# Splitting a unit's value products into three runs instead of two

## The chip, the cores and the metric

The kernel runs on one core of one Trainium2 chip. The metric is device time in microseconds: the time of one execution of the whole kernel. Five engines matter here: TensorE (PE in the profile, its weight loads PEld), VectorE (DVE), ScalarE (ACT), GpSimd (POOL) and SyncE (SP), which here issues the transfers.

## The reference

A batch of 4 sequences of 1024 tokens, each with 1024 channels, goes through attention with 16 heads of 64 channels, and then through a causal convolution. All of it is in float32.

```
scale, shift = split(emb @ W_emb + b_emb)
xn     = rms_norm(x, g_norm) * (1 + scale) + shift
q,k,v  = heads(xn @ W_qkv)
q, k   = rms_norm(q, g_q), rms_norm(k, g_k)
attn   = softmax(q @ k.T * d**-0.5)
o      = attn @ v
x      = x + o + o @ W_out          # attention and its residual
out    = x + causal_conv(x, 4 taps from cond) + b
```

What the change touches is the middle: the scores `q @ k.T`, the softmax over the keys, and the product of the weights with `v`, called the value product below.

## The kernel before

**Tiling.** Two heads of 64 channels make a pair and share the 128 partitions. A sequence has 8 pairs. The work on one pair and one half of its queries (512 of 1024) is a *unit*, so there are 4 x 8 x 2 = 64 units, and the main loop at the end of the kernel passes once for each. They are counted from 0 here.

**One unit.** The keys of a sequence are 8 tiles of 128. For each key tile, `Unit.scores` (L629) multiplies keys by queries for both heads, one head in rows 0 to 63 of TensorE and the other in rows 64 to 127, into one PSUM tile `s` of 128 x 1024; the pool of these tiles, `ps_s`, has two buffers. ScalarE copies the tile to SBUF as `sp` (L637), from a pool of nine, and VectorE keeps a running maximum over the tiles, `mx` (L646). When all eight have come, GpSimd takes the maximum over the partitions (L651), ScalarE puts it into PSUM as `mbp` (L660), in a buffer of that same pool of two, VectorE subtracts it from each tile (L665), ScalarE takes the exponential (L669), and GpSimd adds the tiles up as `sum` (L671). `Unit.values` (L692) then multiplies the eight tiles of weights by `v` into one PSUM tile `pav`, both heads side by side in TensorE's columns. `Unit.finish` (L707) multiplies `sum` by ones for the totals `tot`. The totals go through a scratch in DRAM and come back as reciprocals, by which `divide` (L747) scales `pav`.

**Overlap of units.** The softmax of a unit takes long on VectorE, ScalarE and GpSimd. So a unit's value products stand in the next pass of the loop, between the scores of the next unit: `last` is the unit before. In each pass the scores go out in four groups of two key tiles. After each group `fill()` runs a stretch of other work that is due: products of the projections to q, k and v (L589, a scheme with seven products in place of eight), of the output projection (L881, L950), transposes, loads and stores. `split` cuts this work into four stretches. It puts what lies within the last 26 us by its estimate (20 in the first sequence) into the fourth stretch, after the scores, so in most passes the first three stretches hold nothing.

**What sets the order.** The order of TensorE's instructions is that of the calls in the main loop. The other engines' instructions are issued through `defer(delay, key, step)`: a step is put on a list with a due time on the planner's own clock, and `tick(us)` moves that clock and runs what has come due. `scores` and `values` tick by `PAIR`, 0.9, for each key tile. So where calls change places, the clock stands elsewhere between them, and steps that come due there are issued at another place of their engine's queue. Among the deferred steps are those of `Pair`: `squares` (L437, ScalarE), `sums` (L443, VectorE), `root` (L446, a square root on ScalarE, with a load of its table) and `scale` (L451, VectorE), which normalise q and k of a coming pair. [...] Semaphores keep data and buffers safe.

**Buffers around the change.** Score tile `kt` needs the buffer of tile `kt - 2` in `ps_s`, so it waits for ScalarE's copy of that tile. The copy into `sp` number `kt` takes, in the pool of nine, the place of tile `kt - 1` of the unit before, so it needs that unit's value product `kt - 1` to be done.

Of the kernel before, what the change touches and what calls it, by code (L numbers as in the profile page):

```python
# [21 lines left out]
def kernel(  # L22
# [36 lines left out]
    NT = N // P  # L59
    HN = N // 2  # L60
    HT = NT // 2
# [34 lines left out]
    def defer(delay, key, step):  # L96
        pending.append((clock[0] + delay, next(serial), key, step))
# [42 lines left out]
    def need(*key):  # L140
        flush(lambda e: e[2] == key)
# [616 lines left out]
    def gather(b, half):  # L758

        for kh in range(2):  # L760

            n = KH - kh if b == B - 1 else KH
            for k in range(n):
                need("oT", b, kh * KH + k, half)
            if half:
                four = apool.tile([P, 8, QN], F32, tag="r", name=f"ob_{b}_{kh}_{half}", bufs=2)
                four = four.rearrange("p i t -> p (i t)").rearrange("p (k t) -> p k t", t=HN)
            else:
                four = apool.tile([P, KH, HN], F32, tag="ob", name=f"ob_{b}_{kh}_{half}", bufs=2)
            nc.sync.dma_start(four[:, :n, :], scrO[b][half][:, kh * KH : kh * KH + n, :])  # L770
            for k in range(n):
                oTs[b, kh * KH + k, half] = four[:, k, :]
# [403 lines left out]
    def between(p):  # L1176

        b, i = divmod(p, NB)
        slots = [[] for _ in range(7)]
        for j in range(7):  # L1180
            T = 7 * (p + 4) + j
            slots[j] = piece(T) if T < ND * NPR + 16 else []
        slots[0].append((0.0, lambda: store(AGE)))
        d, k = divmod(p - 11, NB)
        if 0 <= d < B - 1 and k % 2 == 0 and k < NJ:
            slots[0].append((0.0, lambda: OutSums(d, k // 2).load()))
        for a, g in enumerate(range(products_until(p), products_until(p + 1))):
            slots[(2, 5)[a]] += out_product(g)
        if p in REST_PLAN:
            at = sum(n for q, n in REST_PLAN.items() if q < p)  # L1190
            for m in REST[at : at + REST_PLAN[p]]:
                slots[6] += [(0.0, lambda: store(AGE_REST))] + out_pieces(m)
                slots[6].append((0.0, lambda m=m: late.append((clock[0], outs[m].store))))
        return [piece for slot in slots for piece in slot]

    def cut(pieces, shares):

        ends = list(accumulate(shares))
        total = sum(t for t, _ in pieces)
        stretches, done = [[] for _ in shares], 0.0  # L1200
        for t, step in pieces:
            at = (done + t / 2) / max(total, 1e-9) * ends[-1]
            stretches[next((i for i, e in enumerate(ends) if at < e), len(ends) - 1)].append((t, step))
            done += t
        return stretches

    def run(pieces):
        for t, step in pieces:
            until = clock[0] + t
            step()  # L1210
            if until > clock[0]:
                tick(until - clock[0])

    def split(pieces, behind):

        left, n = behind, len(pieces)
        while n and left > 0:
            n -= 1
            left -= pieces[n][0]
        return cut(pieces[:n], SHARES) + [pieces[n:]]  # L1220
# [30 lines left out]
    last = None  # L1251
    for p in range(B * NB):
        unit = Unit(doubles[p // 4].pairs[p // 2 % 2], p % 2)
        stretches = split(between(p), BEHIND if p >= NB else BEHIND_FIRST)
        if p == B * NB - 1:


            gather(B - 1, 0)
            gather(B - 1, 1)
            stretches = cut(between(p), SHARES) + [own]  # L1260
        stretches = iter(stretches)

        def fill():
            run(next(stretches))

        unit.scores((0, 1))
        if last is not None:
            need("exp", last.name)
            last.values(range(0, HT))
        fill()  # L1270
        unit.scores((2, 3))
        fill()
        unit.scores((4, 5))
        if last is not None:
            last.values(range(HT, NT))
            last.finish()
        fill()
        unit.scores((6, 7))
        need("mx", unit.name)
        unit.softmax()  # L1280
        if last is not None:
            defer(2.7 if p > B * NB - 2 else DIVIDE, ("oT", last.pr.b, last.pr.c, last.half), last.divide)
        fill()
        last = unit
# [46 lines left out]
```

## Time and profile before

| what | value |
|---|---|
| time, median of 3 runs | 2895.81 us (2890.95 to 2898.24) |
| the profiled execution | 2907.69 us, span of the profile 2905.7 us |
| TensorE clock granted | 0.99 |
| busy: PE, DVE, ACT, POOL | 2793.5, 2182.2, 1695.1, 1345.1 us |
| value products (L692) | 2048 matmuls, 605 ns mean |
| scores (L629) | 2048 matmuls, 623 ns mean |
| score copies (L637) | 512, 1016 ns mean |
| running maxima (L646) | 448, 1328 ns mean for the 384 after the first of each unit |
| subtraction (L665) | 512, 1213 ns mean |
| product for q, k, v (L589) | 3504 matmuls of 128x384, 493 ns mean |

The profile is of one execution on the chip. Times are in microseconds unless marked ns. A float32 matmul shows as two records, so a score tile of two heads is four records. Matmuls are pipelined and their ends are modelled, so lengths of neighbours overlap by up to 0.16 us; the distance from start to start is the better measure. A timeline line gives the start, the length, the engine, the line of the kernel, the operation, output<-inputs, the shape, and how many instructions were merged; brackets hold the engine's idle time before it and what ended that. In a list of waits, a line gives who waited for whom, microseconds in total, times, and the longest.

### The profile page before, as it was taken

How to read it: one execution, taken by the hardware profiler on the slowest of the kernel's cores; microseconds unless marked ns; L12 is line 12 of the kernel's file. 1: busy time of each engine (PE TensorE's matmuls, PEld its weight loads, DVE VectorE, ACT ScalarE, POOL GpSimd, SP SyncE). 2: the span in 40 equal slices, each digit the busy share in tenths (PEclk: the TensorE clock that was granted, in tenths of full speed). 3: DMA queues.
4: the chain of work that ended last, by engine and by line, in shares of the span. 5: the costliest groups of instructions: out<-in, count | busy, mean ns of one | idle time of the engine just before them, and what ended most of it. 6: DMA issues, size and time to landing. Idle time of an engine off the chain costs nothing.

```text
span 2905.7 us, 32179 instructions
## 1 busy us (share of the span) xinstructions
PE 2793.5 (96%) x10529; PEld 1317.5 (45%) x10529; DVE 2182.2 (75%) x2652; ACT 1695.1 (58%) x2269; POOL 1345.1 (46%) x534
## 2 busy tenths in 40 slices
PE   7999999999999999999999999999999999999999
PEld 3544444444444544544444444454444444444344
DVE  3578878888878776787787777787787868788763
ACT  3165657765556666665565666765565656556532
POOL 1045555555455544445544553544553555545520
PEclk9999999999999999999999999999999999999999
DMA  7864455755445656655655564765565445432433
GB/s 278 286 203 135 151 169 177 226 171 163 140 151 189 210 163 199 217 178 186 203 173 166 191 201 141 238 210 179 181 215 172 145 147 178 151 111 87 131 105 116
DMA packets 416255, 510.98 MB, mean 176 GB/s; under 512 B 41889, under 2 KB 327897, under 8 KB 406361
## 3 DMA queue, kind: packets, MB, share of 16 engines
q1 hardware_dynamic: 416088, 508.93, 54.0%
q8 instruction: 84, 1.38, 0.2%
q14 instruction: 83, 0.67, 0.1%
HBM read 413.43 MB, written 95.40 MB: 175 GB/s over the span
## 4 chain that ended last, share of the span: by engine, by line
PE 69%; DVE 14%; ACT 7%; DMA 5%; issue 3%; POOL 1%; SPq 1%; DVEq 0%; ACTq 0%; POOLq 0%
PE pqkv_P L589 27%; PE pav L692 14%; PE s L629 13%; PE po L950 5%; DVE mx L646 5%; PE po_P L881 4%; PE po L881 3%; ACT sp L637 3%; DVE sp L665 3%; ACT sp L669 2%; DMA scrR<-few 1%; DMA rec<-scrR 1%; DVE r L321 1%; PE qkt L459 1%; PE tot L707 1%
## 5 line engine op out<-in xcount | busy, mean ns | idle before, releaser
L589 PE MATMUL pqkv_P<-w_P,a 128*128 128x384 f32 x3504 | 1198.2, 493 | 29.3 <-issue 9.3
L671 POOL TENSOR_TENSOR sum<-sum,sp 128x1024 f32<-128x1024 f32 x384 | 956.1, 2490 | 62.1 <-ACT sp L669 31.6
L589 PEld LDWEIGHTS pqkv_P<-w_P,a 128*128 128x128 f32 x3504 | 652.0, 191 | 505.5 <-issue 91.8
L637 ACT COPY sp<-s 128x1024 f32<-128x1024 f32 x512 | 512.6, 1016 | 489.1 <-PE s L629 385.8
L646 DVE TENSOR_TENSOR mx<-mx,sp 128x1024 f32<-128x1024 f32 x384 | 510.0, 1328 | 174.6 <-ACT sp L637 146.3
L665 DVE TENSOR_TENSOR sp<-sp,mbp 128x1024 f32<-128x1024 f32 x512 | 605.0, 1213 | 18.1 <-ACT mbp L660 18.1
L669 ACT ACTIVATE sp<-sp 128x1024 f32<-128x1024 f32 x512 | 527.6, 1056 | 147.2 <-DVE sp L665 143.1
L651 POOL PARTITION_ALL_REDUCE mb<-mx x64 | 220.5, 3445 | 839.0 <-DVE mx L646 662.6
L629 PE MATMUL s<-qT,kT 64*128 64x512 f32 x2048 | 519.7, 623 | 38.0 <-ACT sp L637 22.8
L692 PE MATMUL pav<-sp,v 128*64 128x512 f32 x2048 | 473.9, 605 | 0.0
L671 POOL TENSOR_TENSOR sum<-sp,sp 128x1024 f32<-128x1024 f32 x64 | 151.3, 2364 | 493.3 <-ACT sp L669 218.9
L629 PEld LDWEIGHTS s<-qT,kT 64*128 64x128 f32 x2048 | 170.0, 186 | 337.9 <-issue 172.6
L692 PEld LDWEIGHTS pav<-sp,v 128*64 128x64 f32 x2048 | 137.2, 138 | 322.0 <-issue 314.3
L986 DVE SCALAR_TENSOR_TENSOR y<-x,cols,y 128x512 f32<-128x512 f32 x192 | 248.0, 1296 | 46.8 <-ACT y L974 42.2
L646 DVE TENSOR_TENSOR mx<-sp,sp 128x1024 f32<-128x1024 f32 x64 | 110.5, 1727 | 104.2 <-ACT sp L637 104.2
L608 DVE TENSOR_TENSOR qk<-u,pqkv_P 128x256 f32<-128x256 f32 x256 | 106.8, 417 | 89.7 <-PE pqkv_P L589 85.3
L950 PE MATMUL po<-ob,wo 128*128 128x512 f32 x352 | 155.3, 593 | 0.0
L881 PE MATMUL po_P<-o_P,wq_P 128*128 128x512 f32 x320 | 143.9, 592 | 0.0
L660 ACT COPY mbp<-mb 128x1024 f32<-128x1024 f32 x64 | 65.2, 1019 | 116.5 <-POOL mb L651 116.4
L451 DVE TENSOR_TENSOR qk<-qk,ms 128x1024 f32<-128x1024 f32 x64 | 125.9, 1968 | 2.2
L881 PE MATMUL po<-o_P,wq_P 128*128 128x512 f32 x240 | 108.0, 592 | 0.0
L437 ACT ACTIVATE sq<-qk 128x512 f32<-128x512 f32 x128 | 76.7, 629 | 52.2 <-DVE qk L608 48.1
(96 smaller groups left out, 1886.2 us busy)
## 6 DMA issues: line engine op xcount, KB each, us to landing
a<-scrA SPq DMA_DIRECT2D x215, 512.0 KB
w_P<-scrB SPq DMA_DIRECT2D x64, 768.0 KB
o_P<-scrS SPq DMA_DIRECT2D x40, 1024.0 KB
w_P<-in_L_cond_W_qkv_dram SPq DMA_DIRECT2D x144, 256.0 KB
o_P<-scrO SPq DMA_DIRECT2D x30, 1024.0 KB
scrA<-r SPq DMA_DIRECT2D x28, 896.0 KB
wq_P<-scrW SPq DMA_DIRECT2D x70, 256.0 KB
xc<-in_x_dram SPq DMA_DIRECT2D x64, 256.0 KB
```

The source lines that it names most:

```text
L589: nc.tensor.matmul(pm, (chunks[0, k].r(place) if a is None else a[:, k, :])[:, t % 2 * P : (t % 2 + 1) * P], w[:, k, :], start=(k == 0), s ...
L629: nc.tensor.matmul(ps[:, h, :], pr.kT[kt // HT][h * D : (h + 1) * D, kt % HT * P : (kt % HT + 1) * P], pr.qT[self.half][h * D : (h + 1) * ...
L637: nc.scalar.copy(sp, ps)
L646: nc.vector.tensor_max(self.mx, self.mx if kt > 1 else self.sp[0], self.sp[kt])
L651: nc.gpsimd.partition_all_reduce(self.mb.rearrange("p h q -> p (h q)"), self.mx.rearrange("p h q -> p (h q)"), P, bass_isa.ReduceOp.max,)
L665: nc.vector.tensor_sub(self.sp[kt], self.sp[kt], self.mb)
L669: nc.scalar.activation(sp, sp, AF.Exp)
L671: nc.gpsimd.tensor_tensor(self.sum, self.sum if kt > 1 else self.sp[0], sp, ALU.add)
L692: nc.tensor.matmul(self.pav[h * D : (h + 1) * D, :], self.pr.v[kt // HT][:, kt % HT, h * D : (h + 1) * D], self.sp[kt][:, h, :], start=(kt ...
L881: nc.tensor.matmul(pm, self.w[name][:, k, :], self.o[name][:, k, :], start=(k == 0 and name not in ("P2", "P3", "P4")), stop=(k == KH - 1),)
L950: nc.tensor.matmul(self.pm, self.w[kh][:, k % KH, :], oTs[b, k, half], start=False, stop=(k == NJ - 1),)
L986: nc.vector.scalar_tensor_tensor(self.y, self.x1[:, k : k + HN], cols[:, r : r + 1], self.y, ALU.mult, ALU.add)
```

## The change

In each pass with a predecessor, the second half of its value products, tiles 4 to 7, stood in one run behind scores 4 and 5. Tiles 4 and 5 now stand ahead of scores 4 and 5, after the second `fill()`; tiles 6 and 7, and the totals, stay where they were. The first half, tiles 0 to 3, stays behind scores 0 and 1. The last unit, whose value products come after the loop in one run, is as before.

```diff
         fill()
         unit.scores((2, 3))
         fill()
+        if last is not None:
+            last.values(range(4, 6))
         unit.scores((4, 5))
         if last is not None:
-            last.values(range(HT, NT))
+            last.values(range(6, NT))
             last.finish()
         fill()
         unit.scores((6, 7))
```

`HT` is 4 and `NT` is 8. `values` opens the PSUM tile `pav` when its first key tile is 0, and closes the accumulation at tile 7, so a run may be cut anywhere between.

## The prediction

> **What bounds the kernel now.** I read the page first (busy shares, the chain that ended last), then the list of waits, then the timeline of single units in each engine. Units are counted from 0, one per pass of the main loop (64 passes).
>
> ```profile
> span 2905.7 us, 32179 instructions
> PE 2793.5 (96%) x10529; PEld 1317.5 (45%) x10529; DVE 2182.2 (75%) x2652; ACT 1695.1 (58%) x2269; POOL 1345.1 (46%) x534
> ...
> PE 69%; DVE 14%; ACT 7%; DMA 5%; issue 3%; POOL 1%; SPq 1%; DVEq 0%; ACTq 0%; POOLq 0%
> ```
>
> TensorE is busy 96% of the span and carries 69% of the chain; the rest of the chain is mostly VectorE. What TensorE waits for, from the list of waits:
>
> ```profile
> PE s L629 <- ACT sp L637: 22.8, 63, 3.1
> PE s L629 <- DVE sp L665: 15.0, 10, 3.4
> ```
>
> 63 waits of the scores for ScalarE's copies, about one a unit. Where they sit shows in the timeline of TensorE in unit 34 (start, length, then the instructions merged):
>
> ```profile
> 1531.68 1.99 PE L629 MATMUL s<-qT,kT 64*128 64x512 f32 x8
> 1533.60 3.65 PE L692 MATMUL pav<-sp,v 128*64 128x512 f32 x16
> 1537.18 1.99 PE L629 MATMUL s<-qT,kT 64*128 64x512 f32 x8
> 1539.48 2.04 PE L629 MATMUL s<-qT,kT 64*128 64x512 f32 x8 [0.31 <-ACT sp L637]
> 1541.46 3.65 PE L692 MATMUL pav<-sp,v 128*64 128x512 f32 x16
> 1545.04 0.64 PE L707 MATMUL tot<-sum,ones 128*32 128x256 f32 x8
> ```
>
> Score tiles 0 and 1, four tiles of the predecessor's values, score tiles 2 to 5 without a break, four tiles of values, the totals. Tile 4 needs the PSUM buffer of tile 2 (the scores have two), and ScalarE copies it out only at
>
> ```profile
> 1538.42 1.93 ACT L637 COPY sp<-s 128x1024 f32<-128x1024 f32 x2 [2.62 <-PE s L629]
> 1540.71 1.01 ACT L637 COPY sp<-s 128x1024 f32<-128x1024 f32 x1 [0.37 <-PE s L629]
> ```
>
> The first of the two copies ends near 1539.43, and tile 4 starts at 1539.48.
>
> **What the Trainium skill says.** "TensorEngine Tiling (Array Packing)", section Key Properties: changing the tiling mode, not only the tile, drains TensorE. The trace agrees: scores (64*128) and values (128*64) are different modes, and a block costs more than its tiles (below). The same page, section PSUM Bottleneck: tiling speeds TensorE but not the evacuation of PSUM; here a score tile's matmuls take 0.86 us and its copy 1.01. "TensorE: Matmul & The Clock Gate", on engine queue depths: ScalarE and VectorE are strict FIFO. I use this for the copies queued behind a waiting square root; the trace shows ScalarE's instructions in program order.
>
> **The change, part by part.** It moves values 4 and 5 of the predecessor ahead of scores 4 and 5. No instruction is added or removed, and values 6, 7 and the totals stay behind scores 5. Single matmuls in the trace start in pairs, a pair every 0.429 us, two pairs a tile: 0.858. A block of two score tiles lasts 1.92 (1531.68 to 1533.60), so entering and leaving it costs 1.92 - 1.72 = 0.20. Four value tiles last 3.58 (1533.60 to 1537.18): 3.43 and 0.15. Two value tiles then last 1.72 + 0.15 = 1.87.
>
> *An ordinary unit.* Before: scores 2 to 5 4.28 (1537.18 to 1541.46) + values 3.58 = 7.86. After: 1.92 + 1.87 + 1.92 + 1.87 = 7.58. So 0.65 of stall goes, 0.35 of two mode changes comes, 0.28 is left. Tile 4 now starts 3.79 after tile 2, and tile 2's buffer is free 2.25 after it, tile 3's 3.2 after it: neither wait is left, with 1.5 us over. Scores 6 start 3.4 after scores 5, their buffer free after 2.3: no new wait there.
>
> *What is queued behind.* Scores 4 and 5 start 1.5 us later, so their copies (ScalarE) and running maxima 4 and 5 (VectorE) do too. This hides in VectorE's idle time before maximum 6 (2.24 us in unit 34), or under its backlog; in every ordinary unit I worked through, maximum 5 still ends before copy 6 arrives. The copy of tile 5 no longer waits for value 4 (0.91 in unit 34); nothing waited for that copy.
>
> *Where the gain passes.* 63 units have a predecessor. In four (24, 25, 40, 41) a product already stands between scores 3 and 4: no stall to remove; a product-to-values change and a values-to-scores change replace a product-to-scores one, about +0.16 each, +0.6 in all. Of the other 59, eight keep nothing. In 2, 6, 14, 16 and 60 maximum 6 starts late behind VectorE's other work, and the next unit's second score tile waits for VectorE's last subtraction: TensorE arrives earlier and waits longer. In 5 and 63 the totals wait for GpSimd's sum (2.57 and 2.54), and after 62 scores wait 3.10 for ScalarE. Elsewhere TensorE sets the pace, or VectorE's chain starts at copy 6 and moves with it.
>
> *The moved square root.* By the order of ScalarE's instructions in the changed kernel, the square root of the norms (L446, with its table load) moves from behind copies 4 and 5 to ahead of them in units 4, 8, ... 60 (24 and 40 had it there). It waits for VectorE's sums (L443). Unit 52, VectorE and then ScalarE before:
>
> ```profile
> 2301.28 6.38 DVE L986 SCALAR_TENSOR_TENSOR y<-x,cols,y 128x512 f32<-128x512 f32 x3
> 2307.58 1.27 DVE L443 TENSOR_REDUCE ms<-sq 128x8 f32<-128x512 f32 x2
> ```
>
> ```profile
> 2304.78 1.01 ACT L637 COPY sp<-s 128x1024 f32<-128x1024 f32 x1 [0.37 <-PE s L629]
> 2306.70 1.01 ACT L637 COPY sp<-s 128x1024 f32<-128x1024 f32 x1 [0.91 <-PE pav L692]
> 2307.74 1.28 ACT L446 ACT_TABLE_LOAD   x1
> 2309.03 0.31 ACT L446 ACTIVATE ms<-ms,eps 128x16 f32<-128x16 f32 x1
> ```
>
> Unit 52 begins at 2295.75. The sums end 13.1 after that; root 0.31 and copy 4 1.01 end at 14.65, so scores 6, due at 13.64 and formerly at 13.92, start near 14.7: +0.8. Unit 8 (sums at 15.9, scores 6 formerly at 16.3): to 17.3, +1.0. Unit 60 (13.4): +0.9, which falls into the 1.17 that the next unit's scores wait for VectorE anyway. In the other ten of these units the sums end 6.6 to 10.4 after the start; copy 4 is due at 10.5 to 10.9 and has 2 us to spare before scores 6: free.
>
> *Sum.* 59 - 8 - 2 = 49 units x 0.28 = 13.7; four of them (21, 22, 37, 38) stall 0.05 less (-0.2), 9 and 33 stall more (+0.44): 14.0. Less 0.6 and 1.8: **11.5 us off**. The profiled execution took 2907.7 us with a span of 2905.7, 0.4% over the median of 2895.8; a saving of a few tenths in each unit is the same in both. 2895.8 - 11.5 = **2884.3**.
>
> The least certain price is the block of two values, which no trace shows alone. Its lower bound is 1.79, half of the block of four, were the extra mode changes free (gain about 0.43 a unit, 21 us over 49 units, 18 net). Its upper bound: I allow both changes to cost half as much again (0.53), leaving 0.10 a unit, 5 us, 2.5 net. I take 1.87, as the same two changes stand around every block of values.
>
> **The rivals.**
> *Absorbed further.* In units 1 to 18 VectorE and TensorE wait for each other often (the second score tile is late by up to 3.6 us), and a copy that comes 1.5 later can delay a maximum there. If these 18 gave nothing, about 13 x 0.28 = 3.6 less and 1 for unit 8: 7 to 8 us off, 2888; with the dearer mode change 2893. For it: VectorE's 14% of the chain. Against: in ten of those units VectorE idles just before maximum 6 (0.9 to 3.0).
> *More than counted.* Mode changes nearly free, or the relief of copy 5 helps ScalarE: 18 us off, 2878. Against: the 0.20 and 0.15 are in every unit.
> *Slower: the square root holds the copies.* Place: the fifteen units named, ahead of copy 4. Price: for each microsecond that the sums end after 12.3 from the unit's start, scores 6 are one later. It decides when the ten harmless units see their sums at about 13.5 (as in unit 52): 10 x (0.28 + 0.8) = 11, all of the gain. At 14.5 each loses 1.8 rather than gaining 0.28, 21 us: 2884 + 21 = 2905. Against: their sums end by 10.4, and VectorE's order hardly changes (two units in which the sums move earlier).
> *Nothing happens.* Excluded as to order: in every unit with a predecessor, two and two value tiles stand around scores 4 and 5. As to time it is the first rival.
>
> **How the numbers follow.** Forecast (9 to 15 us off, 2881 to 2887) 0.58; more than counted 0.10; absorbed 0.26; slower 0.06. About 0.3%, 8.7 us, is what a measurement can tell from no change: faster 0.58 + 0.10 = 0.68, less 0.01 for the edge: 0.67; same 0.27; slower 0.06. The range for 8 in 10 takes in the absorbed case to 2892 and the nearly free mode change to 2878; the forecast's own range is 2881 to 2887.
>
> **What would show it.** From the start of score tile 2 to that of tile 6: 8.42 before, 8.14 after in ordinary units. Score waits for ScalarE's copies: from 22.8 us in 63 to 6 to 9 in about 8 (unit 0, which has no predecessor, keeps three), a new one of 0.6 to 1.2 in units 8, 52 and 60. Waits of scores for VectorE's subtraction up by 1 to 2 us. A two-tile block of values longer than 1.9, or tile-6 waits in the other ten units of the square root, would make it wrong.

## The result, and the profile after

The changed kernel takes 2882.35 us, median of 6 runs (2878.57 to 2884.86), beside 2896.4 us for 6 runs of the kernel before (2890.95 to 2900.51). The ratio is 0.9951, with a 95% interval of 0.9938 to 0.9964: 14 us less, with an interval of 10 to 18. The forecast was 2884.3, 11.5 us less than the median of 2895.81 that was then known.

The page of the changed kernel, its head and the shares of the chain that ended last:

```profile
span 2881.0 us, 32179 instructions
PE 2790.8 (97%) x10529; PEld 1315.6 (46%) x10529; DVE 2184.3 (76%) x2652; ACT 1684.7 (58%) x2269; POOL 1348.2 (47%) x534
...
PE 74%; DVE 12%; ACT 6%; DMA 4%; issue 3%; POOL 2%; SPq 1%; DVEq 0%; ACTq 0%; POOLq 0%
```

TensorE has as much to do as before and waits less, so its share of the chain grows from 69% to 74%. The two spans differ by 24.7 us, more than the medians: the execution of the kernel before that was profiled was 11 us over its median, and this one (2883.05 us) is close to its own. I come back to that below.

The list of waits (who waited for whom, microseconds in total, times, the longest):

```profile
PE s L629 <- DVE sp L665: 12.4, 9, 2.8
...
PE s L629 <- ACT sp L637: 6.9, 7, 3.5
```

The waits of the scores for ScalarE's copies went from 22.8 us in 63 to 6.9 in 7. Unit 34 shows how, in the timeline of TensorE (start, length, then the instructions merged):

```profile
1520.22 1.99 PE L629 MATMUL s<-qT,kT 64*128 64x512 f32 x8
1522.14 1.94 PE L692 MATMUL pav<-sp,v 128*64 128x512 f32 x8
1524.01 1.99 PE L629 MATMUL s<-qT,kT 64*128 64x512 f32 x8
1525.92 1.94 PE L692 MATMUL pav<-sp,v 128*64 128x512 f32 x8
1527.79 0.64 PE L707 MATMUL tot<-sum,ones 128*32 128x256 f32 x8
```

and in that of ScalarE:

```profile
1521.45 1.93 ACT L637 COPY sp<-s 128x1024 f32<-128x1024 f32 x2 [2.62 <-PE s L629]
1525.24 1.93 ACT L637 COPY sp<-s 128x1024 f32<-128x1024 f32 x2 [1.86 <-PE s L629]
```

From start to start, scores 2 and 3 last 1.92, values 4 and 5 1.87, scores 4 and 5 1.91, values 6 and 7 1.87: the four numbers of the prediction's working. The second of the two copies that scores 4 and 5 need ends at 1523.38, and scores 4 start at 1524.01, so no wait is left. From score tile 2 to score tile 6 it is 8.14 (1520.22 to 1528.36), where it was 8.42.

### The profile page after: what moved, and what is told of

It reads as the page before. It is cut to its first block, busy times and chain, and to the rows that moved or that the text cites. A ratio compares the mean times of both kernels' runs of the same rounds, so it can differ in the third digit from the quotient of the medians.

```text
span 2881.0 us, 32179 instructions
## 1 busy us (share of the span) xinstructions
PE 2790.8 (97%) x10529; PEld 1315.6 (46%) x10529; DVE 2184.3 (76%) x2652; ACT 1684.7 (58%) x2269; POOL 1348.2 (47%) x534
## 4 chain that ended last, share of the span: by engine, by line
PE 74%; DVE 12%; ACT 6%; DMA 4%; issue 3%; POOL 2%; SPq 1%; DVEq 0%; ACTq 0%; POOLq 0%
PE pqkv_P L589 28%; PE s L629 14%; PE pav L692 14%; PE po L950 5%; PE po_P L881 4%; DVE mx L646 4%; PE po L881 3%; DVE sp L665 2%; ACT sp L669 2%; ACT sp L637 1%; PE qkt L459 1%; PE tot L707 1%; DMA rec<-scrR 1%; DVE r L321 1%; DMA scrR<-few 1%
## 5 line engine op out<-in xcount | busy, mean ns | idle before, releaser
L589 PE MATMUL pqkv_P<-w_P,a 128*128 128x384 f32 x3504 | 1192.9, 491 | 27.7 <-issue 9.9
L589 PEld LDWEIGHTS pqkv_P<-w_P,a 128*128 128x128 f32 x3504 | 649.8, 191 | 500.3 <-issue 85.8
L637 ACT COPY sp<-s 128x1024 f32<-128x1024 f32 x512 | 505.6, 1016 | 467.9 <-PE s L629 417.2
L629 PE MATMUL s<-qT,kT 64*128 64x512 f32 x2048 | 516.3, 620 | 19.5 <-DVE sp L665 12.4
L692 PE MATMUL pav<-sp,v 128*64 128x512 f32 x2048 | 487.0, 608 | 0.0
L629 PEld LDWEIGHTS s<-qT,kT 64*128 64x128 f32 x2048 | 174.8, 186 | 311.1 <-issue 200.8
L692 PEld LDWEIGHTS pav<-sp,v 128*64 128x64 f32 x2048 | 131.4, 138 | 333.1 <-issue 323.2
L608 DVE TENSOR_TENSOR qk<-u,pqkv_P 128x256 f32<-128x256 f32 x256 | 106.4, 416 | 82.5 <-PE pqkv_P L589 80.7
```

Of the source, the lines that this page charges most:

```text
L589: nc.tensor.matmul(pm, (chunks[0, k].r(place) if a is None else a[:, k, :])[:, t % 2 * P : (t % 2 + 1) * P], w[:, k, :], start=(k == 0), s ...
L629: nc.tensor.matmul(ps[:, h, :], pr.kT[kt // HT][h * D : (h + 1) * D, kt % HT * P : (kt % HT + 1) * P], pr.qT[self.half][h * D : (h + 1) * ...
L637: nc.scalar.copy(sp, ps)
L692: nc.tensor.matmul(self.pav[h * D : (h + 1) * D, :], self.pr.v[kt // HT][:, kt % HT, h * D : (h + 1) * D], self.sp[kt][:, h, :], start=(kt ...
```

## The experiments

Distances between score tiles are from start to start in the trace of TensorE. "The middle" of a unit is from score tile 2 to score tile 6.

**Both kernels once more.** Without an edit, to see which differences belong to one execution.

> The kernel before once more, unchanged, for a second profile. Theory (TensorE's order decides, the rest is run to run): from unit 20 on, start to start of score tiles 2 and 6 is 8.42 us in ordinary units as in the first profile; what differs from the first profile lies in units 0 to 19 and in stretches of 3.4 us at half clock after a long wait. If the extra gains of the changed kernel in units 23, 31, 35 and 39 (0.8 to 1.7 us each) belong to the change, this profile shows the long times of the first one there; if they are run to run, some of them are gone here too.

> The changed kernel again, without an edit. Theory: 2882 again, 14 us below the kernel before; from score tile 2 to tile 6 8.14 in the same units as in its first profile. What belongs to the one execution that was profiled, and not to the change, differs: the stretches at half of TensorE's clock lie elsewhere and in another number (9 to 13 of them in the executions of the two kernels so far), and the differences in units 13 to 19, 31 and 35 between the first two profiles don't return alike. Rival (those differences belong to the change): they return in the same units with the same sizes.

The kernel before took 2896.98 us in its second profiled execution. The changed kernel took 2881.28 us (5 runs, 2879.42 to 2883.78) beside 2897.04 for the kernel before (11 runs), ratio 0.9945 (0.9927 to 0.9962). The middles of the ordinary units are 8.42 and 8.14 again, to 0.01; only unit 2 of the changed kernel was at 8.43 in the first profile, where the totals waited 0.22 for GpSimd's sum. Much of what is large outside the middles did not return. Unit 31 began with 1.79 from score tile 0 to 1 in the first profile of the kernel before, and with 0.96 in the second; the end of unit 23 is 1.7 shorter in the second; unit 47 begins with 3.26 in the second profile of the changed kernel, and with 0.96 in its first and in both of the kernel before. Two of the units named beforehand did keep a difference. Score tile 0 to 1 of unit 35 is 1.65 and 1.35 in the two profiles of the kernel before and 0.96 in both of the changed kernel; it is 1.12 to 1.72 in three of the kernels below, so it does not go with the change. The end of unit 39 is 1.7 longer in both profiles of the kernel before: TensorE waits 2.0 for VectorE (L608) there in all four profiles, and a stretch at half of its clock follows in those two alone. The last section comes back to it. The second profiled executions (2896.98 and 2881.28) lie at the medians, so they are the pair to divide: their spans are 2894.9 and 2879.2, 15.7 apart. This is where the 15.7 lie, worked out unit by unit:

| part of the second pair of profiles | difference, us |
|---|---|
| middles of 48 ordinary units | -13.4 |
| middles of units 33 and 61 | -1.0 |
| middles of units 4 and 16 | -0.3 |
| middles of units 9, 24, 25, 40, 41, +0.15 each | +0.8 |
| middles of units 8, 52, 60 | +2.0 |
| middles of units 5, 6 and 63 | -4.7 |
| all that lies outside the middles | +1.0 |

The row of units 5, 6 and 63 can't be booked as a gain of the change: against the first profile of the kernel before, the three together differ by 0.0. The last row is a sum of pieces of up to 2.6 with both signs. Most of them don't repeat; what stands in the pair of first profiles too is -1.7 in unit 39, -1.2 and -1.4 in unit 5, -0.5 in unit 52 and +0.3 and +0.5 in unit 59.

**One change of mode more or less.** In the first, values 4 and 5 and scores 4 and 5 alternate singly:

```diff
-        if last is not None:
-            last.values(range(4, 6))
-        unit.scores((4, 5))
+        for kt in (4, 5):
+            if last is not None:
+                last.values((kt,))
+            unit.scores((kt,))
```

> The changed kernel, with values 4 and 5 apart: value 4, score 4, value 5, score 5, values 6 and 7. One more score block and one more value block in each of 63 units, no stall more or less. Theory (a block of scores costs 0.20 and a block of values 0.15 beside its tiles): +0.35 us in each unit, score tile 2 to tile 6 from 8.14 to 8.49 us in ordinary units, about 50 x 0.35 = 17 us slower than the changed kernel, so about 2899, equal to or slightly over the kernel before. Rival (the mode changes are nearly free and the stall alone counts): 8.14 to 8.2 us and 2882 to 2886.

2903.36 us (9 runs, 2894.94 to 2909.4), ratio to the kernel before 1.002 (1.0006 to 1.0035): 21 us more than the changed kernel, which turns the gain into a small loss. Unit 34, TensorE:

```profile
1537.49 1.08 PE L692 MATMUL pav<-sp,v 128*64 128x512 f32 x4
1538.50 1.13 PE L629 MATMUL s<-qT,kT 64*128 64x512 f32 x4
1539.56 1.08 PE L692 MATMUL pav<-sp,v 128*64 128x512 f32 x4
```

A value tile alone takes 1.01 and a score tile alone 1.06, so 0.15 and 0.20 over the 0.858 of their matmuls, the prices that the blocks of four and of two gave. The middle is 8.49 in all ordinary units, 0.35 more than in the changed kernel. No wait is in it; the time is lost on the changes of mode alone. The sum over all middles is 19.2 more than in the first profile of the changed kernel.

In the second, value 4 alone stands ahead of scores 4 and 5, and values 5 to 7 behind:

```diff
-            last.values(range(4, 6))
+            last.values((4,))
         unit.scores((4, 5))
         if last is not None:
-            last.values(range(6, NT))
+            last.values(range(5, NT))
```

> The changed kernel, with value 4 alone ahead of scores 4 and 5, and values 5 to 7 behind. The number of blocks is the same; what stands between scores 3 and 4 is half as long (0.86 + 0.15 us). Tile 2's buffer is free 2.25 us after tile 2 starts; tile 4 comes 0.96 + 0.96 + 1.0 = 2.9 us after it. Theory: no stall is left and tile 2 to tile 6 is 8.14 us as with two tiles; time 2882 +- 4. Rival (it takes two tiles to give ScalarE enough time): a wait for the copy stays in most units, 0.2 us or more, and the time is 2890 or more.

2882.2 us (8 runs, 2878.97 to 2890.5), ratio 0.9957 (0.9943 to 0.997). Unit 34, TensorE:

```profile
1520.35 1.08 PE L692 MATMUL pav<-sp,v 128*64 128x512 f32 x4
...
1523.28 2.79 PE L692 MATMUL pav<-sp,v 128*64 128x512 f32 x12
```

One value tile 1.01, three 2.73 (1523.28 to the totals at 1526.01): the same 0.15 each. The middle is 8.14 in every ordinary unit but unit 2 (8.53, with a wait of 0.32 of the totals for GpSimd's sum). One tile, 1.01 long, is enough to cover the copy; the second adds nothing to the cover and costs nothing. So the price of a block of values does not depend on its length, from one tile to four, nor that of a block of scores, from one tile to two.

That the price goes with the change of mode, and not with any change from one product to another, the kernel before shows. From its first profile, TensorE, all in the mode 128*128:

```profile
1513.09 3.60 PE L881 MATMUL po_P<-o_P,wq_P 128*128 128x512 f32 x8
1516.52 0.60 PE L459 MATMUL qkt<-ident,qk 128*128 128x128 f32 x4
1516.96 7.91 PE L589 MATMUL pqkv_P<-w_P,a 128*128 128x384 f32 x24
```

From start to start the first block takes 3.43, which is 8 x 0.429, the pace of its single matmuls. The third takes 7.74 (the next block starts at 1524.70), which is 24 x 0.3225, again the pace of the single ones. So nothing is added where one product follows another in one mode.

**The same number of blocks elsewhere.** Values 0 and 1 behind scores 1, values 2 and 3 behind scores 3, values 4 to 7 behind scores 5:

```diff
-            last.values(range(0, HT))
+            last.values(range(0, 2))
...
-            last.values(range(4, 6))
+            last.values(range(2, 4))
         unit.scores((4, 5))
         if last is not None:
-            last.values(range(6, NT))
+            last.values(range(4, NT))
```

> Values 0 and 1 of the predecessor behind scores 1, values 2 and 3 behind scores 3, values 4 to 7 and the totals behind scores 5: three blocks of values as in the changed kernel, and so as many changes of mode, in another order of sizes. Theory (the price goes by blocks, the stall is gone wherever value tiles stand between scores 3 and 4): a unit's eight score and eight value tiles take as long as in the changed kernel; score tile 1 to 2 takes 1.9 less, tile 5 to 6 1.8 more, tile 3 to 4 2.8; no wait of the scores for ScalarE in the middle of a unit; the time within 3 us of 2882. Rival (where the blocks stand matters: scores 2 come 1.8 us earlier and meet buffers that copies 0 and 1 still hold): a wait of 0.3 to 0.5 at score tile 2 in every unit, 15 to 25 us more, 2900. Rival on the other side (the middle of the unit waits less for VectorE, which gets its running maxima earlier): 1 to 5 us better than 2882, in units 1 to 18.

2884.33 us (6 runs, 2880.7 to 2889.53), ratio 0.9955 (0.9939 to 0.9972); the changed kernel in the same comparison 2881.28 and 0.9945. Unit 34, TensorE:

```profile
1523.69 1.94 PE L692 MATMUL pav<-sp,v 128*64 128x512 f32 x8
...
1531.26 3.65 PE L692 MATMUL pav<-sp,v 128*64 128x512 f32 x16
```

From units 20 to 62 score tile 0 to 2 is 1.72 shorter and the middle 1.72 longer in nearly every unit, 0.00 in sum. So the time goes by the number of blocks, and not by where they stand, as long as one stands between scores 3 and 4. The wait at score tile 2 that the first rival wanted in every unit stands in two, 23 and 39 (0.38 and 0.46); units 4 and 16 have one of 0.37 at score tile 3. The second rival's gain in units 1 to 18 did not come either: from the start of unit 0 to that of unit 20 this execution loses 7.8 us on the first profile of the changed kernel. Whether they are the order's or the execution's, one profile can't say; the medians, 3 apart, have overlapping intervals.

**The square root where it was.** The root of the odd pairs' first halves is due 1.8 later on the planner's clock, which puts it behind copies 4 and 5 again:

```diff
                 delay += LATER[self.c % 2][g]
+                if step == self.root and self.c % 2 and g == 0:
+                    delay += 1.8
```

> The changed kernel, with the square root of the norms (L446) of the first half of each odd pair due 1.8 later, so that it stands behind the copies of tiles 4 and 5 again, as before the change. Theory (the moved root delays copy 4, and through it scores 6, in units 52 and 60 only): the score waits of 0.69 in unit 52 and 0.94 in unit 60 go, both units show 8.14 from score tile 2 to tile 6; waits of scores for ScalarE fall from 6.9 us in 7 to about 5 in 5; the time is 0.7 us better (unit 60's part falls into a wait that stands anyway): 2881.5, which no median can tell from 2882.3. Rival (the root costs in more units than those two): other units of the square root shorten too, in sum by several us: 2877 to 2879. Other rival (the later root delays the scaling behind it, and through it the loads or products that wait for it): longer by 2 us or more, with new waits of products.

2881.45 us (6 runs, 2877.54 to 2889.19) beside 2881.28 for the changed kernel. The list of waits (this kernel is two lines longer, so L629 is L631 here):

```profile
PE s L631 <- ACT sp L639: 4.8, 5, 3.1
```

The waits in units 52 and 60 are gone, as expected, and the middles of both are 8.14 (8.90 and 9.15 in the changed kernel). But in units 8 and 52 nothing is won with it. In unit 52 the stretch after score tile 6 is 0.78 longer instead: there the products (L589) now wait 0.72 for VectorE (`ou`, L900), a wait that stood in the kernel before with 0.41 and is absent in the changed kernel, which comes there later. In unit 8 the transposes (L305) wait 1.37 for VectorE, 0.21 in the second profile of the changed kernel, and start 31.2 after the unit's start in both. So in these two units the wait that the change brought was hidden by one further on. Unit 60 stays open: its 1.06 comes back as 0.80 in unit 61 against the first profile of the changed kernel, and not at all against the second, where the second score tile of unit 61 waited 1.05 for VectorE (0.47 in the first, 0.95 here). Units 52, 60 and 61 together are 0.2 shorter than in the first profile and 1.1 shorter than in the second, where 0.7 was expected; the medians show nothing.

**Another cover for the copy.** The kernel before, with a product of a projection between scores 3 and 4 in place of value tiles, taken from the fourth stretch of the pass:

```diff
-        return cut(pieces[:n], SHARES) + [pieces[n:]]
+        head, tail = cut(pieces[:n], SHARES), pieces[n:]
+        if not any(t for s in head for t, _ in s):
+            k = next((i for i, (t, _) in enumerate(tail) if t >= 2), -1) + 1
+            head[1], tail = sum(head, []) + tail[:k], tail[k:]
+            head[0], head[2] = [], []
+        return head + [tail]
```

> The kernel before with its values in two runs of four, and in passes whose first three stretches were empty the first projection product of the last stretch is put between scores 3 and 4 instead. Theory (anything of over 0.5 us between scores 3 and 4 takes the stall away): the waits of scores for copies of tile 2 are gone in those units; a product block between scores costs 0.19 for the product and 0.20 for the second score block, so 0.65 - 0.39 = 0.26 us is gained in each unit, nearly as in the changed kernel. But scores 4 to 7 and with them the softmax come 2.6 us later while the work that covers the softmax is 2.6 us shorter, so in the units where the next scores wait for VectorE this wait grows by up to 2.6 us: 2884 if few units are bound that way, 2900 or more if many are. Rival (it was the earlier value products that helped, not the gap between scores): score tile 2 to tile 6, less the product's 2.6, stays at 8.4.

2986.49 us (4 runs, 2976.98 to 2994.28), ratio 1.0311 (1.0284 to 1.0338): 89 us slower than the kernel before. What the theory said of one unit holds: unit 34, TensorE,

```profile
1569.05 1.99 PE L629 MATMUL s<-qT,kT 64*128 64x512 f32 x8
1570.97 2.85 PE L589 MATMUL pqkv_P<-w_P,a 128*128 128x384 f32 x8
1573.75 1.99 PE L629 MATMUL s<-qT,kT 64*128 64x512 f32 x8
```

has no stall; the middle is 2.34 longer and the rest of the unit 2.63 shorter, 0.29 won, in units 34, 36, 46 and others. What it left out is large. By unit 19 this execution is already 31 us behind the second profile of the kernel before: in 16 of the units 1 to 18 the second score tile waits for ScalarE's copy of the first, 23.0 us in all, where the kernel before has one such wait, of 1.1, in unit 18. Why it waits there was not followed up. In the units after that the last scores come 2.3 us later than before and the stretch that covers the unit's softmax is shorter by that, so the second score tile of some later units waits for VectorE (units 23, 31, 35, 39, 47 and 51; score tile 0 to 1 in unit 31 is 0.96 in the second profile of the kernel before, 3.57 here). In units 60 to 62 the nearest product lay behind transposes of the output (L997), which came along and held the scores up, 19.3 of the 23.0 us in the second line below; 23.0 of the 29.4 us in the first are those of units 1 to 18:

```profile
PE s L629 <- ACT sp L637: 29.4, 23, 3.4
PE otp L997 <- DVE y L986: 23.0, 8, 6.3
```

Against the same profile the execution is 51 us behind at unit 60 and 97 after unit 63. Thirty stretches at half of TensorE's clock, 138 us in all, where that profile has 9 with 42 us, also carry part of it, up to 48 us (half of the 96 between). How the loss divides among these, this one profile doesn't tell. What it shows is that the gap alone removes the stall, without earlier value products, and that a product taken from the end of the pass is no good cover in this kernel.

## Why the prediction was right, and where not

**The gain of an ordinary unit: right.** 0.65 of stall removed, 0.35 of two mode changes added, 0.28 left; measured 0.28 to 0.29, in 44 of the 48 ordinary units (unit 2 in one pair of profiles only). The block of two values, which no trace had shown alone, is 1.87. The page "TensorEngine Tiling (Array Packing)" of the Trainium skill says under Key Properties that a change of mode drains TensorE; the runs put its price here at 0.15 for entering and leaving a block of values and 0.20 for one of scores, at any length.

**The four units with a product between: right.** The middles are longer by 0.15 in 24, 25, 40 and 41, predicted +0.16. Units 21, 22, 37 and 38 won 0.23 and unit 33 won 0.56 to 0.58, as predicted. Unit 9 was a miss of this step: it has transposes (L305) between scores 3 and 4 (1.54 from tile 3 to tile 4 before, 3.41 after), so it lost 0.15, where I had counted 0.42 won.

**The units that keep nothing: not as predicted.** Unit 62 won its 0.28 and, in the second pair of profiles, kept it: the wait for ScalarE behind it only moved along. In unit 14 0.25 of the 0.29 come back in the stretch after score tile 6 in the second profile of the changed kernel, and nothing in the first. Behind unit 2 the wait that was to grow did not: score tile 0 to 1 of unit 3 is 2.79 and 2.93 before, 2.65 and 2.67 after. For 6 and 16 the size can't be told: the wait is different by more than 0.28 between two executions of one kernel (the scores of unit 7 waited 0.44 for the subtraction in one profile of the kernel before, and 1.99 in the other). The same holds for 5 and 63, whose totals wait for GpSimd's sum: the middle of unit 5 is 11.01 and 13.31 before, 10.22 and 9.63 after. The sum of the waits for the subtraction was to rise by 1 to 2 us; it is 15.0 and 14.3 before, 12.4 and 15.4 after, so neither shown nor refuted. Units 4 and 16 won only 0.13 in the middle, since score tile 6 is later there by 0.15.

**The moved square root: the delay right, what it costs wrong.** Unit 52 in the changed kernel, ScalarE and then TensorE:

```profile
2285.26 0.31 ACT L446 ACTIVATE ms<-ms,eps 128x16 f32<-128x16 f32 x1 [3.19 <-DVE ms L443]
2285.48 1.91 ACT L637 COPY sp<-s 128x1024 f32<-128x1024 f32 x2
```

```profile
2286.52 1.61 PE L629 MATMUL s<-qT,kT 64*128 64x512 f32 x6 [0.69 <-ACT sp L637]
```

The unit begins at 2272.12 and the scores start 14.40 later; I had written 14.7. The terms were right and their sum was not: 13.1, 0.31 and 1.01 make 14.42, and not 14.65, so the loss to expect was 0.5 and not 0.8. Unit 60 waits 0.94. Unit 8 shows nothing in the first profile and this in the second of the changed kernel, ScalarE and then TensorE:

```profile
452.41 0.31 ACT L446 ACTIVATE ms<-ms,eps 128x16 f32<-128x16 f32 x1 [3.52 <-DVE ms L443]
```

```profile
453.67 1.61 PE L629 MATMUL s<-qT,kT 64*128 64x512 f32 x6 [1.03 <-ACT sp L637]
```

17.1 after its start at 436.53; I had written 17.3. In the first profile a stretch at half clock fell on the beginning of the unit, and the sums were in time. So the three units are those named, the other twelve lose nothing to it (the 0.15 missing in 4 and 16 stays when the root is put back), and the middles are longer than before by 0.8, 0.5 and 0.7. The step that failed is the next: that units 8 and 52 pass this on, 1.8 in all. In unit 52 the rest is 0.49 shorter. In unit 8 it is 0.83 shorter than in the first profile of the kernel before, in which the unit has no stretch at half clock either: the transposes (L305) waited 1.08 for VectorE there, and 0.21 here. From start to start unit 8 takes 43.17 before and 43.15 after in these two profiles, unit 52 42.97 in both kernels, so neither passes anything on. I had asked what covers the loss in unit 60, and not in 8 and 52. For unit 60 itself the two pairs of profiles differ: the wait in unit 61 that was to take it up falls from 1.17 to 0.47 in the first and goes from 1.02 to 1.05 in the second.

**The sum.** 11.5 predicted, 14.1 and 15.8 measured, with intervals (10 to 18 and 11 to 21) that hold 11.5 as well; the forecast's 9 to 15 holds the first of the two. With the 1.8 of the square root struck out it is 13.3, and with unit 9 put right 12.7; units 62 and 61 add 0.5 (0.28, and 0.47 where 0.28 was counted), which makes 13.2. What of the measurement's remainder belongs to the change can't be told at this size. The rivals: "more than counted" needed mode changes that cost nearly nothing, and the single tiles exclude that, or help from the relief of copy 5, of which the +1.0 outside the middles shows no sign; "absorbed further" put the gain at 8 us or less, below both intervals, but how much units 1 to 18 kept can't be told: 12 of them have their 0.28 in the middle, and from the start of unit 1 to that of unit 19 it is 705.6 and 700.1 before, 694.6 and 693.5 after; "slower" needed the root's sums at 13.5 in ten more units, and none waits there.

## What to carry to other kernels

Where a short pipeline of PSUM buffers stalls TensorE, put a little work that belongs there ahead of the tile that would wait, but price the block first: on this kernel a change of tiling mode and back costs 0.35, so one block of a single tile wins 0.28 against a stall of 0.65, and two lose it all. Count blocks, not tiles. And before a wait that an edit adds is booked as a loss, look for the next wait behind it on the same engine: in units 8 and 52 such a wait came to nothing.

## What the runs showed of the hardware that I had not expected

In these traces TensorE's granted clock falls to half for stretches of 3.41 us, or a multiple of it, but for the last, at the end of the record. In the clock records of the traces there are 8 to 15 of them in an execution of the kernels above other than the one with the product, 39 to 63 us in all. Unit 7 of the changed kernel shows what one costs. Its first profile, with the second score tile after a wait, and then the values:

```profile
404.18 1.65 PE L629 MATMUL s<-qT,kT 64*128 64x512 f32 x4 [1.75 <-DVE sp L665]
405.77 4.78 PE L692 MATMUL pav<-sp,v 128*64 128x512 f32 x16
```

Its second:

```profile
400.18 1.13 PE L629 MATMUL s<-qT,kT 64*128 64x512 f32 x4 [1.69 <-DVE sp L665]
401.24 3.65 PE L692 MATMUL pav<-sp,v 128*64 128x512 f32 x16
```

The same instructions after nearly the same wait, 1.65 longer. The view by windows of the first profile has the granted clock, PEclk, as the third number from the end, 0.50 and then 1.00:

```profile
404.70:408.10 3.40, 3.40 (x10) 0.77 (x8) 1.61 (x5) 0.78 (x2) 3.32 (x2) 0.50 0.89 260
408.20:411.60 3.40, 3.40 (x18) 1.22 (x16) 2.71 (x1) 2.25 (x3) 2.44 (x2) 1.00 0.87 290
```

10 matmuls in 3.40 us, and 18 in the next. The Trainium skill, "TensorE: Matmul & The Clock Gate", Part 1, tells of windows of 3413 ns that run on their own, not started by the kernel, and of half clock after an idle window. The length agrees: in each trace every stretch starts on one grid with steps of 3.413 us. That a whole window must be idle does not. By the clock records and TensorE's instructions (with their modelled ends) in the four profiles of the two kernels, 41 stretches begin; in the 3.413 us before each, TensorE was idle for 1.48 to 3.22 us, and for 1.88 or more before 37 of them. Of the other windows at full clock, none that was followed by full clock had over 1.84. So what counted here is the idle time within one window, and a little over half of it was enough; unit 7, with 1.75 and 1.69, lies at the edge. Unit 39 shows the place of a wait: its 2.0 us fall into one window in the first profile of the kernel before (2.02 idle, then half clock), and in that of the changed kernel a boundary cuts them (1.84, and full clock). No run moved a wait to test it. It fits what separates executions of one kernel: the first profile of the kernel before has 58 us at half clock and its second 42, worth up to 8 of the 10.7 us between them. A gain of 0.28 in each unit is seen in the traces at once; in the times it needed several runs.
